# Table work in a Fourier transform's stage: scalings on ScalarE, the norm's variance product later, table pieces dealt out evenly

## The chip, the cores and the metric

The kernel runs on one core of one Trainium2 chip, in float32. The metric is the device time of one execution in microseconds, as the median of several runs. The trace is that of one execution, taken by the hardware profiler.

A core has five engines, each with its own in-order queue: TensorE (PE) multiplies matrices, VectorE (DVE) and ScalarE (ACT) work element by element, GpSimd (POOL) does the same more slowly and issues transfers, SyncE (SP) issues transfers. They wait for each other on semaphores.

## The reference, cut to what matters

The input `x` is [16, 16, 256, 256]: batch, channels, rows, columns. Two layers follow each other. The second, a convolution block, is not touched by the change. The first is a Laplace neural operator on a group-normalised `x`:

```python
alpha = jnp.fft.fft2(x, axes=(-2, -1))
A = 1.0 / (omega1[:, None, None, None] - weights_pole1[None])
Bm = 1.0 / (omega2[:, None, None, None] - weights_pole2[None])
S = jnp.einsum('ikpq,oikp,xikq->oxik', weights_residue, A, Bm)
output_residue1 = jnp.einsum('biox,oxik->bkox', alpha, S)
C = jnp.einsum('biox,oikp->bikpx', alpha, A)
D = jnp.einsum('bikpx,xikq->bikpq', C, Bm)
output_residue2 = jnp.einsum('bikpq,ikpq->bkpq', D, weights_residue)
x1 = jnp.fft.ifft2(output_residue1, s=(Ny, Nx), axes=(-2, -1)).real
E1 = jnp.exp(weights_pole1[..., None] * tyc)
E2 = jnp.exp(weights_pole2[..., None] * txc)
```

`x1` plus a product of `output_residue2` with `E1` and `E2` is added to `x`. What depends on the poles alone (`A`, `Bm`, `E1`, `E2` and products of them with the residues) does not depend on `x`: these are the tables. They are computed on the chip, in DRAM tensors `td` (residues times `Bm`), `avd` (`A`, in planes) and `ed` (the exponentials).

## The kernel before, in words

Four stages run one after the other: `layer0_forward`, `layer0_mix`, `layer0_back`, `layer1`. All that is changed lies in `layer0_forward` and in `tables`, which it calls. `layer0_mix` reads `td` and `avd`, `layer0_back` reads `ed`.

**Steps.** The forward transform has 64 steps, one for each of 16 batches times four groups of four channels. Step i does the following. `fetch` has loaded the four channels two steps before, and VectorE has taken their statistics (L174, L176). `halves` of the next step makes the group norm's numbers and `eo`, the sums and differences of the upper and the lower half of the rows: one on VectorE (L191), one on POOL (L194). `rows` runs twice, for two channels each; it multiplies `eo` with the Fourier matrix of the rows (`pu`, L207) and with the first poles' table (`pv`, L214). ScalarE copies one half of `pu` (`right`, L222), VectorE adds and subtracts it (`u`, L224), and ScalarE scales `pv` by the norm's factor `rs` (`v`, L231). `poles` multiplies `v` with the second poles' table (`pd`, L241); VectorE multiplies with the residues (L252), and POOL sums up. `columns` then transforms the columns of the batch before: products `px` (L313), evictions with a scale on ScalarE (`o`, L320), and stores issued by POOL (L329). Three groups of channels have two calls of `columns` with four evictions, the fourth has three calls with five. At a batch's end `finish` closes the residues' sums (L278, L286).

**The norm.** `group_norm_scalars` is a generator with two products on TensorE: the mean (L34), from which VectorE makes the negative mean and the squares `q` (L36 to L39), and, after a `yield`, the variance (L42), followed by an addition (L44), a square root on ScalarE (L46, which needs its own table set) and six small VectorE operations up to `rs` (L53). `halves` runs through it and yields at the same places; the main loop calls `next` before the first `rows`, between the two `rows`, and after the second.

**Tables.** `tables` is one generator. It makes first 16 residue pieces (one for each k: six VectorE operations of 256 columns, L415 to L420, eight small ones, L426, and then four products on TensorE, an eviction and a store), then 33 plane pieces in eleven triples (ten VectorE operations each, L466 to L490, and a store), then 16 exponential pieces (arguments L515, reduction L517 to L522, a sine on ScalarE L523 with its own table set, scaling L525, the exponential by a polynomial L769 to L783, and the rest to L534, with a store). From step 4 on, the loop asks for one piece at the end of each step, 43 in all; the last is asked for at step 46.

**What sets the order.** The block runs under `tc.manual_schedule` for TensorE alone: its instructions stand in the program's order. Those of VectorE, ScalarE, POOL and SP are put in order by a planner, which works with priorities and estimated durations and can run ahead of the program's order when an engine seems free. Semaphores come from data and buffer dependencies. Tables have one buffer for each tile name (`tp`, `bufs=1`); `pu`, `pv` and `px` have two PSUM buffers each; `z` three, `eo` two.

Of the kernel before, what the change touches and what calls it, by code (L numbers as in the profile page):

```python
# [18 lines left out]
C = 16  # L19
# [53 lines left out]
def layer0_forward(ctx, tc, d, al, bd, tabs):  # L73
# [105 lines left out]
    def halves(b, cg, z, mv):  # L179
# [5 lines left out]
        yield from group_norm_scalars(nc, sm, psn, ones, mv, 2, nm, rs)  # L185
# [9 lines left out]
        yield eo, rs  # L195

# [139 lines left out]
    with tc.manual_schedule(engines={mybir.EngineType.PE}):  # L336
# [3 lines left out]
        *_, ready = halves(*steps[0], *fetched.pop(0))  # L340
        pieces = tables(ctx, tc, d, psx, tabs)
        acc = rsc = None
        for i, (b, cg) in enumerate(steps):
            now, following = ready, iter(())
            if i + 1 < len(steps):
                following = halves(*steps[i + 1], *fetched.pop(0))
                next(following)
            v0 = rows(b, cg, 0, *now)
            next(following, None)
# [3 lines left out]
            ready = next(following, None)  # L353
# [5 lines left out]
            poles(cg, (v0, v1), acc)  # L359
            if b:  # L360
                for g0 in range(8 * cg, 8 * cg + 8 if cg < 3 else NF, 4):
                    columns(b - 1, g0, rsc)
            if i + 2 < len(steps):
                fetched.append(fetch(*steps[i + 2]))
            if i >= 4:
                next(pieces, None)
# [16 lines left out]
def tables(ctx, tc, d, psum, tabs):  # L383
# [5 lines left out]


    krow = load(nc, cp, d["krow_t"], [P, N], "krow_t")
    w = frequencies(nc, cp, d["tx"], krow, [P, N], "wt")
    sign = load(nc, cp, d["sign_t"], [P, 1], "sign_t")
    qr = cp.tile([P, C], F32, name="tqr")
    qi = cp.tile([P, C], F32, name="tqi")
    rr = cp.tile([P, C, M], F32, name="trr")
    ri = cp.tile([P, C, M], F32, name="tri")
    for t in range(2):
        ps = slice(64 * t, 64 * t + 64)
        nc.sync.dma_start(out=qr[ps], in_=d["p2r_iq"])  # L400
        nc.sync.dma_start(out=qi[ps], in_=d["p2i_iq"])
        nc.sync.dma_start(out=rr[ps], in_=d["rr_iq"])
        nc.sync.dma_start(out=ri[ps], in_=d["ri_iq"])
    nc.vector.tensor_scalar(qi, qi, sign, None, ALU.mult)
    nri = cp.tile([P, C, M], F32, name="tnri")
    nc.vector.tensor_scalar(nri, ri, sign, None, ALU.mult)
    nc.vector.tensor_scalar(ri, nri, -1.0, None, ALU.mult)
    q2 = cp.tile([P, C], F32, name="tq2")
    nc.vector.tensor_tensor(q2, qr, qr, ALU.mult)
    mt = load(nc, cp, d["mt"], [P, 2, 16], "mt")  # L410
    for k in range(C):
        e = tp.tile([P, N], F32, tag="te", name="te")
        r = tp.tile([P, N], F32, tag="trec", name="trec")
        br = tp.tile([P, N], F32, tag="tbr", name="tbr")
        nc.vector.tensor_scalar(e, w, qi[:, k : k + 1], None, ALU.add)  # L415
        nc.vector.tensor_tensor(r, e, e, ALU.mult)
        nc.vector.tensor_scalar(r, r, q2[:, k : k + 1], None, ALU.add)
        nc.vector.reciprocal(r, r)
        nc.vector.tensor_scalar(br, r, qr[:, k : k + 1], -1.0, ALU.mult, ALU.mult)
        nc.vector.scalar_tensor_tensor(e, e, -1.0, r, ALU.mult, ALU.mult)  # L420
        wts = []
        for h in range(2):
            wt = tp.tile([P, 2, 2, 16, M], F32, tag=f"wt{h}", name="wt")
            shape = [P, 16, M]
            for part, c, coef in ((0, 0, rr), (0, 1, ri), (1, 0, nri), (1, 1, rr)):
                nc.vector.tensor_tensor(  # L426
                    wt[:, part, c],
                    mt[:, h].unsqueeze(2).to_broadcast(shape),
                    coef[:, k].unsqueeze(1).to_broadcast(shape),
                    ALU.mult,  # L430
                )
            wts.append(wt)
        yield
        ps = psum.tile([P, 2, N], F32, tag="px", name="pt")
        for h, wt in enumerate(wts):
            for part, rhs in ((0, br), (1, e)):
                nc.tensor.matmul(
                    ps[:, h],
                    lhsT=wt[:, part].rearrange("p c i m -> p (c i m)"),
                    rhs=rhs,  # L440
                    start=part == 0,
                    stop=part == 1,
                )
        t = tp.tile([P, 2, N], F32, tag="tt", name="tt")
        nc.scalar.copy(t, ps)
        nc.sync.dma_start(out=td[:, :, k], in_=t)

    krow = load(nc, cp, d["krow_m"], [P, N], "krow_m")  # L450
    w = frequencies(nc, cp, d["ty"], krow, [P, N], "wm")
    sign = load(nc, cp, d["sign_m"], [P, 1], "sign_m")
    pr = cp.tile([P, 32], F32, name="tpr")
    pi = cp.tile([P, 32], F32, name="tpi")
    for q in range(4):
        nc.sync.dma_start(out=pr[32 * q : 32 * q + 32], in_=d["p1r_ip"])
        nc.sync.dma_start(out=pi[32 * q : 32 * q + 32], in_=d["p1i_ip"])
    nc.vector.tensor_scalar(pi, pi, sign, None, ALU.mult)
    pr2 = cp.tile([P, 32], F32, name="tpr2")
    nc.vector.tensor_tensor(pr2, pr, pr, ALU.mult)  # L460
    npr = cp.tile([P, 32], F32, name="tnpr")
    nc.vector.tensor_scalar(npr, pr, -1.0, None, ALU.mult)
    for g in range(NF):
        four = [P, 32, 4]
        e = tp.tile(four, F32, tag="ae", name="ae")
        nc.vector.tensor_tensor(  # L466
            e,
            w[:, 4 * g : 4 * g + 4].unsqueeze(1).to_broadcast(four),
            pi.unsqueeze(2).to_broadcast(four),
            ALU.add,  # L470
        )
        r = tp.tile(four, F32, tag="ar", name="ar")
        nc.vector.tensor_tensor(r, e, e, ALU.mult)
        nc.vector.tensor_tensor(r, r, pr2.unsqueeze(2).to_broadcast(four), ALU.add)
        nc.vector.reciprocal(r, r)
        av = tp.tile([P, 32, 4, 3], F32, tag="av", name="av")
        half = [64, 32, 4]
        nprb = npr.unsqueeze(2)
        nc.vector.tensor_tensor(av[:64, :, :, 1], r[:64], nprb[:64].to_broadcast(half), ALU.mult)
        nc.vector.tensor_tensor(av[64:, :, :, 1], r[64:], e[64:], ALU.mult)  # L480
        nc.vector.scalar_tensor_tensor(
            av[:64, :, :, 0].rearrange("p k f -> p (k f)"),
            e[:64].rearrange("p k f -> p (k f)"),
            -1.0,
            r[:64].rearrange("p k f -> p (k f)"),
            ALU.mult,
            ALU.mult,
        )
        nc.vector.tensor_tensor(av[64:, :, :, 0], r[64:], nprb[64:].to_broadcast(half), ALU.mult)
        nc.vector.tensor_scalar(av[:, :, :, 2], av[:, :, :, 0], -1.0, None, ALU.mult)  # L490
        nc.sync.dma_start(out=avd[g], in_=av.rearrange("p k f l -> p (k f l)"))
        if g % 3 == 2:
            yield


    phase = load(nc, cp, d["phase"], [P, 1], "phase")
    turn = cp.tile([P, 1], F32, name="turn")
# [4 lines left out]
    for i, axis in enumerate("12"):  # L502
# [7 lines left out]
        for k in range(0, C, 2):  # L510
# [16 lines left out]
            if axis == "2":  # L527
                nc.vector.tensor_scalar(n, n, last, None, ALU.mult)
# [971 lines left out]
```

## Time and profile before

| | |
|---|---|
| median of three runs | 7309.22 us (7302.86 to 7325.03) |
| profiled execution, its own time | 7312.28 us |
| its span | 7310.5 us |
| forward transform in it, up to the first matmul of the mix | 1384.24 us |
| PE / PEld / DVE / ACT / POOL busy | 6750.3 / 3787.1 / 4970.2 / 3811.4 / 3470.0 us |
| granted TensorE clock, mean over the span | 0.969 of full speed |

In the forward transform (the first 1376 us) the groups of instructions that the change touches are these. Times are busy times in us over the stage, and means in ns of one.

| line | engine, tile | count | busy | mean |
|---|---|---|---|---|
| L42 | PE, `gn_var` | 128 | 22.5 | 245 |
| L46 | ACT, `gnr` | 64 | 13.0 | 203 |
| L46, L523 | ACT, loads of a table set | 17, 16 | 21.8, 20.5 | 1283 |
| L415, L417, L419 | DVE, residue scalings of 256 columns | 16 each | 5.4, 7.6, 5.8 | 336, 475, 365 |
| L490 | DVE, third plane, 128 columns | 33 | 11.7 | 356 |
| L515, L525 | DVE, arguments' scalings of 256 columns | 32 each | 10.4, 10.1 | 341, 351 |
| L528 | DVE, last scaling of 512 columns | 8 | 3.8 | 479 |
| L437 | PE, `pt` | 128 | 39.7 | 405 and 379 |
| L207, L214 | PE, `pu` and `pv` | 2048 each | 426.8, 413.3 | 292, 285 |
| L222 | ACT, `right`, 256 columns | 256 | 95.0 | 372 |

Float32 products show as two matmul records for each instruction of the program. A page's row gives the busy time of a group and, beside it, how long the engine had been idle just before its members and what ended that. An engine that is busy nine tenths of a slice sets the pace there; one that has two or three tenths does not, unless others wait for it. In an answer on waits the columns are the engine and line that waited, what it waited for, us in total, times, and the longest.

### The profile page before, as it was taken

The numbers are of one execution on the slowest core, as the hardware profiler recorded it, in microseconds if no ns is written. First come the engines' busy times: TensorE is split into PE (matmuls) and PEld (weight loads), VectorE is DVE, ScalarE is ACT, GpSimd is POOL, SyncE is SP. The second block draws the span as 40 slices with busy tenths as digits, with TensorE's granted clock in tenths as the row PEclk, the third lists the DMA queues.
The fourth block names the chain that finished last, engine by engine and source line by source line (L and its number), as shares of the span: only waits on it lengthen the run. The fifth ranks groups of instructions, "written<-read, shape, count | busy, mean of one in ns | idle before, by whom it ended". The sixth has DMA issues, their size and how long they took to land.

```text
span 7310.5 us, 147410 instructions
## 1 busy us (share of the span) xinstructions
PE 6750.3 (92%) x57640; PEld 3787.1 (52%) x57640; DVE 4970.2 (68%) x9465; ACT 3811.4 (52%) x5915; POOL 3470.0 (47%) x4612
## 2 busy tenths in 40 slices
PE   7889999899999998999789999999999999999997
PEld 5777778666667776777433333333333333333332
DVE  8999975466666665888666666666666666666662
ACT  2223333466666665222366666666666666666662
POOL 2334445322222222666554666556665555655663
PEclk9889999999999999999899999999999999999998
DMA  3344444433333333999767888888888888888886
GB/s 100 112 115 125 119 125 125 124 100 97 96 94 98 99 99 107 321 327 326 227 195 218 249 256 257 249 259 248 267 260 243 253 248 268 253 247 254 252 267 219
DMA packets 716089, 1443.59 MB, mean 197 GB/s; under 512 B 98954, under 2 KB 525254, under 8 KB 673638
## 3 DMA queue, kind: packets, MB, share of 16 engines
q1 hardware_dynamic: 567206, 959.76, 43.8%
q0 software_dynamic: 148192, 474.40, 20.9%
q8 instruction: 460, 7.54, 0.4%
q14 instruction: 231, 1.89, 0.1%
HBM read 877.12 MB, written 556.47 MB: 196 GB/s over the span
## 4 chain that ended last, share of the span: by engine, by line
PE 71%; DVE 16%; DMA 4%; ACT 4%; issue 3%; POOL 1%; SPq 0%; DVEq 0%; ACTq 0%; POOLq 0%
PE c2ps L1173 18%; PE c L1029 12%; PE pd L1097 12%; PE ph L700 5%; PE ps L643 5%; PE pg L665 4%; PE px L313 3%; ACT wide L1077 3%; DVE alb L607 2%; PE pu L207 2%; PE pr L1056 2%; PE py L860 2%; PE pv L214 2%; PE py L861 2%; DVE u L224 2%
## 5 line engine op out<-in xcount | busy, mean ns | idle before, releaser
L1077 ACT ACTIVATE wide<-c,b 32x512 f32<-32x512 f32 x2176 | 1479.3, 680 | 354.2 <-PE c L1029 302.6
L1105 DVE TENSOR_TENSOR t<-pd,r 64x512 f32<-64x512 f32 x1088 | 744.3, 684 | 1287.8 <-PE pd L1097 1262.3
L1108 DVE TENSOR_TENSOR top<-pd,t 32x512 f32<-32x512 f32 x2176 | 1504.1, 691 | 53.7 <-DMA cf<-bot 1.2
L1173 PE MATMUL c2ps<-rows,c 128*32 128x512 f32 x12288 | 1391.9, 600 | 16.4 <-DMA rows<-cf 16.4
L1089 POOL COPY wide<-wide 32x1031 f32<-32x1031 f32 (+1 forms) x576 | 569.6, 989 | 1236.2 <-ACT wide L1077 1208.7
L1029 PE MATMUL c<-z,w 102*128 102x512 f32 x2048 | 1014.5, 628 | 139.2 <-ACT wide L1077 116.6
L1097 PE MATMUL pd<-wide,dw 128*128 128x512 f32 x2048 | 1013.1, 617 | 6.0 <-ACT r L1065 2.9
L1173 PEld LDWEIGHTS c2ps<-rows,c 128*32 128x32 f32 x12288 | 400.3, 109 | 972.0 <-issue 891.6
L720 POOL DMA_DIRECT2D hd<-h x512 | 324.3, 640 | 1198.7 <-DVE h L713 1174.1
L1029 PEld LDWEIGHTS c<-z,w 102*128 102x128 f32 x2048 | 401.5, 198 | 676.5 <-issue 486.9
L1097 PEld LDWEIGHTS pd<-wide,dw 128*128 128x128 f32 x2048 | 377.1, 194 | 613.6 <-issue 447.5
L1182 ACT ACTIVATE e<-c2ps,b 128x512 f32<-128x512 f32 x256 | 176.0, 687 | 831.1 <-PE c2ps L1173 828.4
L1090 POOL COPY wide<-wide 32x1031 f32<-32x1031 f32 (+1 forms) x576 | 573.0, 995 | 36.1
L700 PE MATMUL ph<-ix,yt 64*128 64x256 f32 x4128 | 502.3, 390 | 7.2 <-issue 6.6
L643 PE MATMUL ps<-tt,lt 128*64 128x256 f32 x4224 | 495.5, 384 | 12.6 <-DMA tt<-td 10.0
L313 PE MATMUL px<-wxn,u 128*64 128x256 f32 x4224 | 481.9, 379 | 8.0 <-ACT o L320 7.9
L207 PE MATMUL pu<-fy,eo 128*128 128x128 f32 x2048 | 426.8, 292 | 26.8 <-DVE u L224 21.8
L700 PEld LDWEIGHTS ph<-ix,yt 64*128 64x128 f32 x4128 | 393.1, 190 | 94.0 <-issue 46.8
L1048 ACT ACTIVATE bot<-c,b 128x512 f32<-128x512 f32 x544 | 344.3, 684 | 175.2 <-PE c L1029 167.9
L873 POOL TENSOR_TENSOR x<-x,o 128x512 f32<-128x512 f32 x256 | 324.4, 1267 | 216.6 <-DVE o L872 198.5
L607 DVE TENSOR_SCALAR alb<-alc,m 128x1024 f32<-128x1024 f32 x330 | 419.9, 1396 | 0.0
L214 PE MATMUL pv<-at,eo 128*128 128x128 f32 x2048 | 413.3, 285 | 0.0
(204 smaller groups left out, 10418.6 us busy)
## 6 DMA issues: line engine op xcount, KB each, us to landing
rows<-cf SPq DMA_DIRECT2D x128, 2176.0 KB
z<-zn SPq DMA_DIRECT2D x768, 257.8 KB
cf<-top POOLq DMA_DIRECT2D x512, 240.0 KB, 7.0
cf<-bot POOLq DMA_DIRECT2D x96, 840.0 KB, 11.6
alc<-al SPq DMA_DIRECT2D x264, 256.0 KB
zn<-zb SPq DMA_DIRECT2D x128, 516.0 KB
o<-zn SPq DMA_DIRECT2D x128, 516.0 KB
z<-in_x SPq DMA_DIRECT2D x64, 1024.0 KB
```

The costliest lines, as they stand in the source:

```text
L207: nc.tensor.matmul(pu[:, xh, e].rearrange("p v m -> p (v m)"), lhsT=lhs, rhs=fy[:, e], start=True, stop=True,)
L313: nc.tensor.matmul(ps[64 * k : 64 * k + 64, :, h], lhsT=u[:, h, part, g0 + j + k].rearrange("p f c -> p (f c)"), rhs=wxn[:, h, part], star ...
L643: nc.tensor.matmul(ps[64 * h : 64 * h + 64, v], lhsT=lt[:, h, k, 1 - v : 3 - v].rearrange("p l f c -> p (l f c)"), rhs=tt[:, h, k], start= ...
L700: nc.tensor.matmul(ph[q][:, e], lhsT=yt[lanes, i].rearrange("p t k -> p (t k)"), rhs=ix[lanes, i], start=n == 0, stop=n == 3,)
L1029: nc.tensor.matmul(ps[:, a], lhsT=w, rhs=z[:k, c : c + 2, 0:N], start=True, stop=True)
L1077: nc.scalar.activation(self.feat[64 - 32 * q : 96 - 32 * q, f, self.groups[g], :H], ps[q][32 * f : 32 * f + 32], AF.Mish, bias=b1[0][32 * ...
L1089: nc.gpsimd.tensor_copy(flat[0:32, f, 1:m], flat[64:96, f, 0 : m - 1])
L1090: nc.gpsimd.tensor_copy(flat[96:128, f, 0 : m - 1], flat[32:64, f, 1:m])
L1097: nc.tensor.matmul(ps, lhsT=dwt if self.tail else dw, rhs=self.feat[:, f, cs, :H], start=True, stop=True,)
L1105: nc.vector.tensor_tensor(t[64:128], ps[:64], self.r[:, cs], ALU.mult)
L1108: nc.vector.tensor_tensor(self.top[32 * f : 32 * f + 32, cs, q], ps[lanes], t[lanes], ALU.add)
L1173: nc.tensor.matmul(ps[32 * j : 32 * j + 32], lhsT=c2[:, blk, dx, :], rhs=t[:, 4 * j + blk : 4 * j + blk + 4, x : x + H], start=(blk, dx) = ...
```

## The change

Three things are changed, all in the forward transform.

1. **Variance product.** `halves` takes only the first part of `group_norm_scalars` before it makes `eo`, and goes through the rest after it has yielded `eo`. The loop takes the first yield before the first `rows` and the second after `poles`. So on TensorE the variance product stands behind the second poles' products of the step, in front of the columns, and not between the two halves of the rows.
2. **Scalings.** Seven of the VectorE operations of the tables become ScalarE activations: two additions of a per-partition number (`Identity` with a bias), and multiplications by a per-partition number or by -1 (`Copy` with a scale). One small VectorE operation is new (`nqr`, once).
3. **Pieces.** `tables` now has three generators, `residues`, `planes` and `exponentials`, whose pieces are merged by their place in their own list. There are 65 pieces, planes one by one. Steps 4 to 63 take one each, and steps 4, 16, 28, 40 and 52 two. The operations inside a piece are otherwise the same.

```diff
@@ halves
-        yield from group_norm_scalars(nc, sm, psn, ones, mv, 2, nm, rs)
+        scalars = group_norm_scalars(nc, sm, psn, ones, mv, 2, nm, rs)
+        next(scalars)
...
         yield eo, rs
+        yield from scalars
@@ layer0_forward, main loop
-        *_, ready = halves(*steps[0], *fetched.pop(0))
+        ready, _ = halves(*steps[0], *fetched.pop(0))
...
-                next(following)
+                ready = next(following)
             v0 = rows(b, cg, 0, *now)
-            next(following, None)
             if b and cg == 0:
                 rsc = finish(b - 1, acc)
             v1 = rows(b, cg, 1, *now)
-            ready = next(following, None)
...
             poles(cg, (v0, v1), acc)
+            next(following, None)
...
-            if i >= 4:
+            for _ in range(0 if i < 4 else 2 if i % 12 == 4 else 1):
                 next(pieces, None)
@@ tables: residues()
+        nqr = cp.tile([P, C], F32, name="tnqr")
+        nc.vector.tensor_scalar(nqr, qr, -1.0, None, ALU.mult)
...
-        nc.vector.tensor_scalar(e, w, qi[:, k : k + 1], None, ALU.add)
+            nc.scalar.activation(e, w, AF.Identity, bias=qi[:, k : k + 1])
...
-        nc.vector.tensor_scalar(r, r, q2[:, k : k + 1], None, ALU.add)
+            nc.scalar.activation(r, r, AF.Identity, bias=q2[:, k : k + 1])
...
-        nc.vector.tensor_scalar(br, r, qr[:, k : k + 1], -1.0, ALU.mult, ALU.mult)
+            nc.scalar.activation(br, r, AF.Copy, scale=nqr[:, k : k + 1])
@@ tables: planes()
-        nc.vector.tensor_scalar(av[:, :, :, 2], av[:, :, :, 0], -1.0, None, ALU.mult)
+            nc.scalar.activation(av[:, :, :, 2], av[:, :, :, 0], AF.Copy, scale=-1.0)
...
-        if g % 3 == 2:
-            yield
+            yield
@@ tables: exponentials()
-                nc.vector.tensor_scalar(arg[:, j], tr, pi[:, k + j : k + j + 1], None, ALU.mult)
+                    nc.scalar.activation(arg[:, j], tr, AF.Copy, scale=pi[:, k + j : k + j + 1])
...
-                nc.vector.tensor_scalar(arg[:, j], tr, pr[:, k + j : k + j + 1], None, ALU.mult)
+                    nc.scalar.activation(arg[:, j], tr, AF.Copy, scale=pr[:, k + j : k + j + 1])
...
-                nc.vector.tensor_scalar(n, n, last, None, ALU.mult)
+                    nc.scalar.activation(n, n, AF.Copy, scale=last)
@@ tables: end
+    parts = ((residues(), C), (planes(), NF), (exponentials(), C))
+    order = sorted(((i + 0.5) / n, p) for p, (_, n) in enumerate(parts) for i in range(n))
+    for _, p in order:
+        next(parts[p][0])
         yield
+    for part, _ in parts:
+        for _ in part:
+            pass
```

## The prediction

> **What bounds the kernel now.** I read the page's slices first, to see where in the span the changed code runs. All of it runs in the forward transform, the first seven and a half of the 40 slices (one slice is 7310.5 / 40 = 183 us).
>
> ```profile
> PE   7889999899999998999789999999999999999997
> DVE  8999975466666665888666666666666666666662
> ACT  2223333466666665222366666666666666666662
> PEclk9889999999999999999899999999999999999998
> ```
>
> VectorE (DVE) is at nine tenths in slices 1 to 4, then falls to 7, 5, 4. ScalarE (ACT) has two or three tenths throughout. The granted TensorE clock is lower in slices 1 and 2. So the stage begins bound by VectorE and ends bound by TensorE.
>
> The chain of waits repeats itself in time, so I took step boundaries from the first matmul of the second poles (`pd`, L241) in the timeline: step 5 begins at 163.9, step 36 at 851.3, step 62 ends at 1332.6. Busy times in those windows (columns: window, length, then busy us and count of PE, PEld, DVE, ACT, POOL, then clock, DMA share, GB/s):
>
> ```profile
> 1075.80:1283.10 207.30, 207.30 (x2031) 172.03 (x2030) 121.45 (x375) 68.25 (x136) 107.68 (x150) 1.00 0.45 121
> 163.90:851.30 687.40, 603.80 (x5375) 503.10 (x5374) 635.52 (x1774) 221.50 (x399) 284.22 (x389) 0.94 0.43 119
> 851.30:1332.60 481.30, 467.75 (x4545) 386.74 (x4544) 334.60 (x942) 168.37 (x318) 241.09 (x334) 1.00 0.43 116
> ```
>
> The first line is twelve steps with no table work left: PE is busy all the time, 207.3 / 12 = 17.28 us a step (three of 16.66, one of 19.09), and DVE needs 121.45 / 12 = 10.12. In steps 5 to 35 a step takes 687.4 / 31 = 22.2 us, 20.5 of it DVE; DVE is idle 51.9 us in all, 1.7 a step. Steps 36 to 62 are PE-bound except ten that still carry exponentials (481.3 against 27 bare steps at 464).
>
> Why does DVE idle where it bounds? The waits of 163.9 to 1040.1:
>
> ```profile
> PE gn_var L42 <- DVE gnq L39: 62.6, 21, 5.3
> PE pu L207 <- DVE u L224: 20.2, 20, 1.9
> PE px L313 <- ACT o L320: 7.2, 4, 1.9
> ...
> DVE u L224 <- ACT right L222: 25.8, 27, 1.5
> DVE arg L515 <- DMA ed<-arg: 17.0, 7, 3.6
> DVE arg L525 <- ACT n L523: 10.5, 12, 1.8
> ```
>
> PE's largest wait is the norm's variance product, which stands in the middle of a step's row products and needs a DVE result that is queued behind table work. While PE waits there, it makes no `pu`; afterwards DVE waits for the copy of the next `pu` (25.8 us). The timeline at such a place:
>
> ```profile
> 286.44 0.49 PE L42 MATMUL gn_var<-gnq,ones 128*128 128x2 f32 x2 [4.26 <-DVE gnq L39]
> 286.99 0.77 PE L207 MATMUL pu<-fy,eo 128*128 128x128 f32 x2
> ...
> 290.72 0.39 PE L207 MATMUL pu<-fy,eo 128*128 128x128 f32 x2
> ```
>
> After 4.26 us of waiting the pairs start 0.43 us apart and reach 0.22 only from 290 on.
>
> **What the Trainium skill says.** "TensorE: Matmul & The Clock Gate", section "HAM oscillation — how this bites in real kernels": gaps of more than about 3.4 us put the array back to half rate. The pairs above, 0.43 against 0.22 us, and the mean clock of 0.94 in steps 5 to 35 against 1.00 later agree. "SBUF — State Buffer", section "Who interferes with whom": VectorE operations with two SBUF inputs or in a two-port mode are shut out while GpSimd works; PE and ACT never are. The trace agrees: L52, 143 ns at best, takes up to 2341 ns, about one `eo` subtraction on POOL (L194, 2433 ns). So a scaling moved to ScalarE also escapes that lock.
>
> **The change part by part.**
>
> *Scalings.* DVE loses, by rows of the groups (us in total): L415 5.4, L417 7.6, L419 5.8, L490 11.7, L515 10.4, L525 10.1, L528 3.8, together 54.8 us of instruction time in 152 instructions net. Neighbours overlap, so it is less in busy time. Rows and medians of all table work in steps 5 to 35 give 349.6 us where the windows show 635.5 - 31 x 10.12 = 321.8: a factor 0.92, so about 50 us. ScalarE gains 112 ops of 256 columns (L222's copy of that size: 372 ns, 42 us), 33 of 128 columns and 8 of 512 (about 0.3 and 0.63 us: 15 us). It is busy 221.5 of 687.4 us there, so its 57 us lie in idle time; without that cover they would cost 0.9 us a step. No table-set load is added: the built program has 33 in this stage, as before, 1283 ns each.
>
> *Spreading.* The diff puts one piece a step, but only PE keeps program order; on DVE the planner decides. In the built program it still runs ahead: plane pieces are done by step 27, exponentials by step 35 (before: 19 and 45); only residue pieces, tied to their PE products, reach step 62. With the same medians, table work falls on DVE as follows: steps 0 to 4, 15.6 us (before 10.2); steps 5 to 35, 333.0 (349.6); steps 36 to 62, 32.6 (72.5). So the gain is no halving of a bound: a heavy block (steps 5 to 19, 231.7 to 179.5 us) is levelled into a lighter one.
>
> *The variance product.* It goes behind the sixteen `pd` products, with columns (6.9 us of `px` for four) before the next step's rows. PE stops waiting for `gnq` in the rows. Added is a new order on ScalarE: the square root (L46) now stands before the step's evictions of `px`. If DVE is late with `gnv`, four evictions queue behind it, and PE, having two `px` buffers, stops after 3.5 us of columns; the next `gn_mean`, and DVE's `gnq`, wait in turn. Likewise L422 (needs DVE's square) stands before `right`, and the arguments' scaling (L521) waits for the table's store (3.5 to 3.9 us on the chain) with `right` behind it; it used to be DVE that waited there (17.0 us).
>
> *Sums, against the profiled span.* Steps 5 to 35: DVE busy 31 x 10.12 + 0.92 x 333.0 = 620 us, 20.0 a step; PE needs 17.5. Idle is the unknown. Below, 0: 620 us. Above, with the present 1.7: 673. From the waits, DVE loses about 60 us in the 41 steps to 1040, 1.45 a step; without the 25.8 of the row stalls it is 0.85, and I add something for ScalarE's new round trips: 1.0 a step, 651 us, a gain of 36. Steps 36 to 62: PE bound, 464 + 7.5 residue pieces x 0.86 (eight products of 256 columns at 0.108, px's 6.91 us for 64) = 470.5, a gain of 11. Steps 0 to 4 are DVE-bound and get 5.4 us more table work: a loss of 5. Sum: 42 us faster.
>
> *Costed at nothing.* DMAs: as many stores as before (33 plane, 16 residue, 16 exponential) on SP's queue, but residue stores now stand before later input fetches. A fetch is two steps ahead of use, which hides it; if a store blocks the queue it costs up to the 5.8 us of one late `z`. The last residue product and its store come before nine columns (26 us of `px`), so the next stage's load, issued at 1375 and awaited 10.0 us, stays where it is. Instructions of later stages are unchanged in order.
>
> **The rivals.**
> 1. *The stall only moves.* ScalarE's in-order waits (L46 before evictions, L422 and L521 before `right`) give DVE back what the rows gave: idle 1.7 to 2.3 a step, 673 to 691 us. With +11 and -5 that is 2 to 20 us faster: no change to speak of. For it: 146 or so new crossings; 0.3 us each would be 44 us. Against: in the built order one to three other DVE instructions, 0.8 us or more, stand between most requests and their use.
> 2. *PE becomes the bound.* With the clock at 1.00, steps 5 to 35 near DVE's 620 us and port collisions fewer: 60 to 80 us faster, 7229 to 7249.
> 3. *Slower.* The same square root, but in a loop: DVE late with `gnv`, evictions late, columns stop, `gn_mean` late, DVE dry before `gnq`, gap over 3.4 us, half rate again. It loses 22 us once steps 5 to 35 take 687 + 22 + 11 - 5 = 715, i.e. idle of 95 / 31 = 3.1 us a step, twice today's. From two table loads behind `gnv` (2 x 1.28) and an eviction that would be reached: 7331 or more. Against: PE holds two column groups in hand, and DVE has four BN statistics of 0.67 us and table work to do meanwhile.
> 4. *The planner's front-loading eats it*: more late planes wait for their store (3.0 us on the chain) because one buffer holds `av`. This belongs to rival 1 in time.
>
> **How the numbers follow.** The profiled run took 7312.3 against a median of 7309.2, within their spread, so I subtract 42 from the median: 7267. A difference under 0.3% (22 us) can't be told from none. Forecast (idle 0.5 to 1.5, 7251 to 7282): 0.60. Rival 1 with 4: 0.22. Rival 2: 0.10. Rival 3: 0.08. Faster is forecast, rival 2 and a little of rival 1: 0.72; same: 0.19; slower: 0.09. The range leaves out rival 3 and the far end of rival 2: 7230 to 7305.
>
> **What would show it.** Right: `gn_var`'s wait for `gnq` near nothing; clock 0.98 or more in steps 5 to 35; DVE near 20 us of 21 a step there; PE full from step 36; exponentials ended by step 35. Wrong: waits of `px` on `o`, or of `o` on the square root, of tens of us; DVE waiting on `te`, `trec` or `arg` from ScalarE; `right` late behind L521; steps 5 to 35 over 673 us.

## The result, and the profile after

The changed kernel takes 7323.11 us (median of 12 runs, 7306.53 to 7338.07), the kernel before in the same comparison 7321.65 us (12 runs, 7302.86 to 7336.68): a ratio of 1.0005 with a 95% interval of 0.9994 to 1.0017. There is no difference. The forecast was 42 us less, and the time lies above the forecast's range.

The profiled execution of the changed kernel has a span of 7311.9 us. Its busy tenths in 40 slices:

```profile
PE   6888999899999998999789999999999999999997
DVE  8998755466666665888666666666666666666662
ACT  2444433466666665222366666666666666656662
PEclk9999999999999999999889999999999999999998
```

Slices 1 to 4 (the first is slice 0) show what was meant: ScalarE has four tenths where it had two or three, VectorE comes down a slice earlier, and the granted clock is nine tenths in slices 1 and 2. Yet the stage isn't shorter. Cut at the same places as in the prediction (first `pd` product of a step, now L243):

| boundary or window | before | after | forecast |
|---|---|---|---|
| step 5 begins | 163.9 | 172.6 | 5 later |
| steps 5 to 35 | 687.4 | 656.7 | 651 |
| steps 36 to 62 | 481.3 | 503.0 | 470.5 |
| first product of the mix | 1384.2 | 1385.0 | 42 earlier |

So 30.7 us were won in steps 5 to 35, and 8.7 lost ahead of them and 21.7 behind. The windows of the changed kernel (window, length, then busy us and count of PE, PEld, DVE, ACT, POOL, clock, DMA share, GB/s); the last is a step without table work:

```profile
172.60:829.30 656.70, 586.12 (x5309) 476.29 (x5308) 603.96 (x1660) 277.06 (x527) 284.58 (x389) 0.97 0.43 122
829.30:1332.30 503.00, 489.05 (x4604) 400.53 (x4602) 290.85 (x894) 167.52 (x332) 237.79 (x334) 0.99 0.41 112
1051.90:1068.80 16.90, 16.90 (x166) 13.96 (x164) 10.20 (x30) 5.58 (x12) 8.02 (x11) 1.00 0.42 111
```

VectorE works 603.96 us in steps 5 to 35, less than the forecast 620, but it idles 52.7 us, 1.7 a step, as before. In steps 36 to 62 PE alone is busy for 489.05 us, where 470.5 were to be the whole length, and a bare step takes 16.90 us instead of 16.66.

The waits of steps 5 to 35 of the changed kernel (us in total, times, longest):

```profile
PE pu L209 <- DVE u L226: 51.6, 24, 4.6
...
DVE u L226 <- ACT right L224: 17.8, 22, 1.8
PE px L315 <- ACT o L322: 16.1, 19, 1.7
```

The wait of `gn_var` for `gnq` (62.6 us in the prediction's list) is gone. In its place PE waits for `u`, that is for a free `pu` buffer, 51.6 us, where that wait came to 20.2 us over a longer window before. No other wait of PE or VectorE is of that size in this window.

Step 46 of the changed kernel, one of the seven of steps 36 to 62 that carry a residue piece, in the timeline (start, us, engine and line):

```profile
1020.99 0.70 PE L442 MATMUL pt<-tbr,wt 128*128 128x256 f32 x2
...
1021.52 0.59 PE L442 MATMUL pt<-te,wt 128*128 128x256 f32 x2
...
1022.16 0.23 DVE L431 TENSOR_TENSOR wt<-mt,trr 128x64 f32<-128x64 f32 x1 [3.86 <-PE pt L442]
...
1022.82 0.28 PE L34 MATMUL gn_mean<-mv,ones 128*128 128x2 f32 x2
...
1025.05 1.75 DVE L423 RECIPROCAL trec<-trec 128x256 f32<-128x256 f32 x1
...
1027.62 1.89 DVE L226 TENSOR_TENSOR u<-pu,right 128x256 f32<-128x256 f32 x4
...
1028.78 0.46 PE L209 MATMUL pu<-fy,eo 128*128 128x128 f32 x2 [2.01 <-DVE u L226]
```

The four `pt` products take from 1020.99 to 1022.82, 1.83 us. VectorE, after 3.86 us without work, begins its next eight `wt` at 1022.16, when `pt` has released their first buffer, and does the rest of the piece (reciprocal included) ahead of its first `u` at 1027.62, while PE fills both `pu` buffers and stops for 2.01 us. Such a step takes 20.9 us against 16.9: a residue piece costs 4.0 us here. The seven steps with a piece take 3.2 to 5.6 us more than bare ones, 30.5 together. The two dearest are steps 50 and 61, with 22.5 us each: their mean granted clock is 0.92, where the other five have 1.00.

And the variance product's new place, in a bare step of the changed kernel, then the same place of the kernel before:

```profile
1051.96 2.04 PE L243 MATMUL pd<-bt,v 128*64 128x128 f32 x32
1053.93 0.38 PE L42 MATMUL gn_var<-gnq,ones 128*128 128x2 f32 x2
1054.24 7.13 PE L315 MATMUL px<-wxn,u 128*64 128x256 f32 x64
```

```profile
1075.82 2.04 PE L241 MATMUL pd<-bt,v 128*64 128x128 f32 x32
1077.68 7.08 PE L313 MATMUL px<-wxn,u 128*64 128x256 f32 x64
```

From `pd` to `px` it is 2.28 us instead of 1.86. Before, the product stood among the row products, and the two starts around it lay 0.37 us apart where 0.22 is usual:

```profile
1088.36 0.39 PE L214 MATMUL pv<-at,eo 128*128 128x128 f32 x2
1088.59 0.28 PE L42 MATMUL gn_var<-gnq,ones 128*128 128x2 f32 x2
1088.73 0.47 PE L207 MATMUL pu<-fy,eo 128*128 128x128 f32 x2
```

In the waits between 103 and 172 us of the changed kernel stands what step 5's late start begins with. The four waits lie in steps 0 to 3, where no batch is complete and there are no columns to transform:

```profile
PE gn_mean L34 <- DVE gnv L44: 6.9, 4, 2.5
```

The second of them, in the timeline:

```profile
118.20 0.38 PE L34 MATMUL gn_mean<-mv,ones 128*128 128x2 f32 x2 [2.55 <-DVE gnv L44]
...
120.28 0.64 PE L216 MATMUL pv<-at,eo 128*128 128x128 f32 x2
120.71 0.63 PE L209 MATMUL pu<-fy,eo 128*128 128x128 f32 x2
```

Soon after this wait of 2.55 us, and after one of 2.01 us at 143.88, the row products start 0.43 us apart instead of 0.22, for 3 to 4 us each time. From 102.6 to 153.8 the mean clock is 0.93; in the same steps of the kernel before it was 1.00. So of the 8.7 us only 4.7 are more idle time of PE; the other 4.0 are more busy time for about as many products.

### The profile page after: what moved, and what is told of

The parts are those of the page before. It is cut to its first block, busy times and chain, and to the rows that moved or that the text cites. A ratio compares the mean times of both kernels' runs of the same rounds, so it can differ in the third digit from the quotient of the medians.

```text
span 7311.9 us, 147432 instructions
## 1 busy us (share of the span) xinstructions
PE 6761.3 (92%) x57640; PEld 3780.1 (52%) x57640; DVE 4894.8 (67%) x9313; ACT 3868.0 (53%) x6068; POOL 3461.9 (47%) x4612
## 3 DMA queue, kind: packets, MB, share of 16 engines
q0 software_dynamic: 148192, 474.40, 20.9%
## 4 chain that ended last, share of the span: by engine, by line
PE 74%; DVE 14%; ACT 4%; issue 3%; DMA 3%; SPq 0%; POOL 0%; DVEq 0%; ACTq 0%; POOLq 0%
PE c2ps L1188 18%; PE c L1044 13%; PE pd L1112 13%; PE ph L715 5%; PE ps L658 5%; PE px L315 4%; PE pg L680 4%; ACT wide L1092 3%; DVE alb L622 2%; PE pu L209 2%; PE pr L1071 2%; PE pv L216 2%; PE py L875 2%; PE py L876 2%; PE pt L696 1%
## 5 line engine op out<-in xcount | busy, mean ns | idle before, releaser
L1188 PE MATMUL c2ps<-rows,c 128*32 128x512 f32 x12288 | 1392.4, 600 | 11.8 <-DMA rows<-cf 11.8
L315 PE MATMUL px<-wxn,u 128*64 128x256 f32 x4224 | 488.0, 381 | 16.6 <-ACT o L322 16.6
L331 POOL DMA_DIRECT2D al<-o x544 | 323.2, 606 | 207.4 <-ACT o L322 188.6
```

The lines of the kernel that those rows point to most:

```text
L315: nc.tensor.matmul(ps[64 * k : 64 * k + 64, :, h], lhsT=u[:, h, part, g0 + j + k].rearrange("p f c -> p (f c)"), rhs=wxn[:, h, part], star ...
L1188: nc.tensor.matmul(ps[32 * j : 32 * j + 32], lhsT=c2[:, blk, dx, :], rhs=t[:, 4 * j + blk : 4 * j + blk + 4, x : x + H], start=(blk, dx) = ...
```

## The experiments

From these readings came the theory: the work was taken away, but what counts is where in a step the rest of it stands. A step has a rows phase (first `pu` to first `pd`), in which VectorE must make the norm's numbers, half of `eo` and eight `u` in time for two `pu` buffers, and a columns phase, in which PE works without VectorE. Summed over steps 5 to 35, the rows phase went from 356.1 to 309.6 us and the columns phase from 331.3 to 347.1. The rivals: the planner's front-loading ate the gain; waits for single buffers; stores in the wrong queue; chance of one profile. Times are given as step 5's start, steps 5 to 35, steps 36 to 62, first product of the mix, in us of one profile; the changed kernel has 172.6, 656.7, 503.0, 1385.0. "Table work" is all that `tables` issues.

### The variance product's place

The changed kernel with part 1 undone:

```diff
             v0 = rows(b, cg, 0, *now)
+            next(following, None)
...
             poles(cg, (v0, v1), acc)
-            next(following, None)
...  halves, and the call behind the second rows, as in the kernel before
```

> The changed kernel with the variance product back between the two halves of the rows; scalings on ScalarE and even pieces stay. Windows by the first second-pole product: changed kernel, steps 5 to 35 took 656.7 us and steps 36 to 62 took 503.0. My theory: the product's old place costs TensorE less in a bare step (16.66 and 19.09 us, not 16.90 and 19.44), so steps 36 to 62 drop by 27 x 0.27 = 7 us to 496; in steps 5 to 35 TensorE waits for the squares again, tens of us, and they take 675 to 700. Rival: that wait was never worth anything because VectorE bounds those steps; then they stay within 5 us of 657 and the whole is 7 us faster than the changed kernel.

Measured: ratio to before 0.9988 [0.9978, 0.9998]; 164.7, 669.6, 489.2, 1374.1. Its steps 36 to 62:

```profile
834.40:1323.60 489.20, 479.12 (x4603) 398.06 (x4602) 300.22 (x906) 170.60 (x337) 238.16 (x334) 1.00 0.43 115
```

The early steps get their 8 us back, steps 36 to 62 another 13.8, about half of it in bare steps (16.66 and 19.09 us again) and the rest in steps with a piece (mostly 19.8, that is 3.1 for a piece), and steps 5 to 35 lose 12.9, less than if the wait for `gnq` had been worth its 62.6 us: that wait returns with 9.1 us only. Net, part 1 makes the stage 11 us slower here, in one profile of each.

Part 1 alone, on the kernel before:

> The kernel before with the variance product behind the second poles and nothing else. The prediction's step: waits of the product for the squares (62.6 us) vanish, VectorE's idle time in steps 5 to 19 falls from 2.1 to about 1 us a step, 15 us. Against it bare steps now cost 0.27 us more, 64 x 0.27 = 17 us. So the forward transform stays within 8 us of 1384. Rival, that the wait held TensorE up for its full 62.6 us: 1340 or less.

Measured: 1.0006 [0.9999, 1.0014]; 177.6, 678.5, 483.4, 1389.1. The same picture: 9 us won in steps 5 to 35, 14 lost ahead of them, 2 behind (bare steps take 16.90 and 19.44 here too).

The changed kernel with the product ahead of the poles' products instead of behind them:

```diff
+            next(following, None)
             poles(cg, (v0, v1), acc)
-            next(following, None)
```

> The changed kernel with the variance product in front of the second poles' products, right after the rows, and not behind them. My theory: 0.24 us a bare step is what a product with 128 columns of weights costs between products with 64 columns; beside the rows' products of 128 columns it costs less, so bare steps fall from 16.90 to 16.66 to 16.75 and steps 36 to 62 to about 497 us; steps 5 to 35 stay within 6 us of 657. Rival: the product costs the same at any place that is not between pv and pu; bare steps stay at 16.90.

Measured: 1.0020 [1.0013, 1.0027]; 166.8, 681.3, 494.0, 1394.3. Bare steps take 16.5 and 19.0, so the price of the place between `pd` and `px` is confirmed, and the early wait is gone. But steps 5 to 35 lose 24.6 us, all in the rows phase (357.8), and the wait for `u` rises to 80.9 us. PE is busy for 586.9 us there, as in the changed kernel, so that the loss is idle time. The planner has put VectorE's work in another order; that this is the cause, and which instruction does the harm, was not settled.

### The scalings

Part 2 undone in the changed kernel (the seven activations are VectorE operations again):

> The changed kernel with the seven scalings back on VectorE; the variance product behind the second poles and even pieces stay. My theory: VectorE gets 50 us of busy time back, nearly all in steps 5 to 35, which take 685 to 700 us, and steps 36 to 62 get 1.2 us more work before the first u of each step with a residue piece, 510 us. Rival: ScalarE's round trips cost what they save; then steps 5 to 35 stay within 8 us of 657 and steps with a residue piece get shorter than 20.9.

Measured: 0.9999 [0.9991, 1.0008]; 175.1, 648.6, 502.6, 1379.4.

```profile
175.10:823.70 648.60, 586.90 (x5309) 479.74 (x5308) 618.67 (x1765) 227.15 (x401) 285.61 (x389) 0.97 0.45 123
```

VectorE works 14.7 us more than in the changed kernel, and the window is 8.1 us shorter. Here the scalings on ScalarE bought nothing: what they save VectorE was lost again elsewhere. The hand-overs between the two engines are the likely place (VectorE's wait for `arg` from ScalarE, 10.5 us in the changed kernel, is gone), but this was not shown one by one.

Part 2 alone, on the kernel before:

> The kernel before with the seven scalings on ScalarE and nothing else. The prediction's step (50 us of VectorE's busy time saved where VectorE bounds): steps 5 to 35 take 650 to 660 us (687.4 before) and the forward transform ends at 1345 to 1360 (1384.2). Rival, that the scalings save nothing because VectorE waits for ScalarE's answers: 1376 or more.

Measured: 0.9987 [0.9979, 0.9995]; 163.8, 684.8, 477.2, 1375.0.

```profile
163.80:848.60 684.80, 603.46 (x5374) 501.08 (x5373) 618.31 (x1679) 275.46 (x537) 283.49 (x389) 0.95 0.43 119
848.60:1325.80 477.20, 466.20 (x4545) 385.65 (x4544) 308.16 (x888) 168.43 (x327) 238.30 (x334) 1.00 0.44 117
```

The busy time saved is the forecast's: 635.5 - 618.3 and 334.6 - 308.2, together 43 us in the two windows, against 50. The stage gets 9 us shorter. The rest becomes idle time of VectorE, part of it in front of results that now come from ScalarE (its wait for `arg` is 20.6 us over the stage, 3.4 the longest).

### The spreading

Part 3 alone, on the kernel before:

> The kernel before with the pieces merged and dealt out and nothing else (scalings on VectorE, variance product between the rows). If levelling VectorE's load is what gains: steps 5 to 35 take 665 to 680 us, steps 36 to 62 some 490 (bare steps at 16.66, with a residue piece at 20 to 21), the forward transform 1370 to 1380. Rival, that it only moves the residues' products from steps where TensorE has time to steps where it has none: 1385 or more.

Measured: 1.0001 [0.9992, 1.0009]; 166.1, 672.5, 493.8, 1383.3. It wins 14.9 in steps 5 to 35 and gives back 12.5 in steps 36 to 62, to which it moves residue pieces.

The changed kernel with every piece held until its own step. A piece's first operation gets a zero made of that step's norm, so that the planner can't run ahead:

```diff
+    def gate(src, shape, name):
+        zero = tp.tile([P, 1], F32, tag=f"{name}z", name=f"{name}z")
+        nc.vector.tensor_scalar(zero, step["now"][:, 0:1], 0.0, None, ALU.mult)
+        t = tp.tile(shape, F32, tag=name, name=name)
+        nc.vector.tensor_scalar(t, src, zero, None, ALU.add)
+        return t
...
-            nc.scalar.activation(e, w, AF.Identity, bias=qi[:, k : k + 1])
+            qk = gate(qi[:, k : k + 1], [P, 1], "rgate")
+            nc.scalar.activation(e, w, AF.Identity, bias=qk)
...  planes and exponentials likewise
```

> The changed kernel with every table piece tied to its step: two tiny VectorE operations a piece add zero times the step's norm to one of its inputs, so the planner can't start it before that step (in the built program plane pieces then end at step 62 and not 27, exponentials at 62 and not 35). Theory A, front-loading: the gain was lost because the planner did not spread; with 16.4 us of VectorE and 18.0 of TensorE in each step, steps 5 to 62 take some 1100 us (1159.7 now), the forward transform to the first product of the mix 1325 to 1340 (1385.0 now). Theory B, the pieces' crossings and bursts cost the same wherever they stand: steps 5 to 62 stay over 1140 us.

Measured: 1.0053 [1.0036, 1.0071]; 169.1, 641.9, 549.9, 1414.3.

```profile
169.10:810.90 641.80, 580.85 (x5309) 470.41 (x5308) 513.09 (x1451) 234.07 (x455) 286.80 (x389) 0.98 0.42 117
810.90:1360.90 550.00, 498.37 (x4606) 403.69 (x4604) 439.76 (x1243) 210.46 (x408) 246.37 (x334) 0.99 0.41 111
```

This is the even load that the change's words promise: VectorE 16.6 and 16.3 us a step, PE 18.7 and 18.5, and neither is full in either window. Yet the stage is 29 us slower. So sums of a step don't decide it, and that front-loading ate the gain is not borne out. The gates are not free, though: VectorE works 58 us more in the two windows than in the changed kernel, in 140 more instructions, and at most 7 us of that had stood in steps 0 to 4. A gate also puts a piece right behind the norm. How much of the 29 us is due to the gates was not measured.

The changed kernel with residue pieces dealt out twice as fast, so that two instead of seven fall into steps 36 to 62:

```diff
-    order = sorted(((i + 0.5) / n, p) for p, ...
+    order = sorted(((i + 0.5) / n / (1 if p else 2), p) for p, ...
```

> The changed kernel with the residue pieces merged at half their places, so that in the built program the last one's VectorE work stands in step 41 and not 62. My theory: a residue piece costs 4.0 us in a TensorE-bound step (1.8 of products, 2.0 of late u), and 4 to 5 pieces fewer stand there, so steps 36 to 62 fall from 503 to 482 to 488; in steps 5 to 35 they cost VectorE 3.9 us each, so these rise by 12 to 20 us from 656.7, and the first product of the mix stays within 10 us of 1385. Rival, that the loss after step 36 comes from the variance product's place alone: steps 36 to 62 stay over 497.

Measured in one execution: 7322.48 us; 175.2, 675.1, 483.9, 1387.3.

```profile
175.20:850.30 675.10, 600.92 (x5351) 490.01 (x5350) 618.23 (x1715) 286.19 (x547) 285.64 (x389) 0.96 0.43 120
850.30:1334.20 483.90, 478.24 (x4565) 390.89 (x4564) 275.43 (x839) 158.40 (x312) 237.75 (x334) 1.00 0.42 113
```

Five pieces fewer make the late window 19.1 us shorter (3.8 a piece) and the early one 18.4 longer (3.7 a piece). A residue piece costs about 3.8 us in either window of the changed kernel. At that price, as an estimate, the eight pieces that the change took out of steps 5 to 35 (16 before, 8 after) come to some 30 us, as much as was won there in all; in exchange the exponentials of the late steps moved in.

### Buffers, and the phase of the work

The changed kernel with two buffers for the residue pieces' tiles:

```diff
-            e = tp.tile([P, N], F32, tag="te", name="te")
+            e = tp.tile([P, N], F32, tag="te", name="te", bufs=2)
...  tbr, wt0 and wt1 likewise
```

> The changed kernel with two buffers each for a residue piece's te, tbr and two wt tiles. My theory: a residue piece in the TensorE-bound steps costs 4 us because VectorE stands idle until the piece before has been multiplied (wt waits for pt, 32.8 us in steps 36 to 62) and then has 5 us of work before the first u; with two buffers that wait falls under 5 us, the step with a piece falls from 20.9 to about 18.7 us (only the products' 1.8 us left), and steps 36 to 62 take about 489 us. Rival: the cost is the products and the queue on ScalarE, not the buffer; then they stay at 500 or more.

Measured: 0.9969 [0.9959, 0.9979]; 174.5, 632.1, 497.9, 1354.9.

```profile
174.50:806.60 632.10, 579.34 (x5309) 468.60 (x5308) 589.13 (x1648) 272.39 (x522) 285.34 (x389) 0.98 0.45 126
```

The stage is 30 us shorter, but not where it was expected. In steps 36 to 62 only 5.1 come back: five of the seven steps with a piece still take 20.2 to 20.3 us, and VectorE's wait for `pt` is still 26.2 us (32.8 with one buffer). Why two buffers leave most of that wait was not found. The gain is 24.6 us in steps 5 to 35. There the rows phase falls from 309.6 to 291.1, PE's wait for `u` from 51.6 to 32.7, and the table work that VectorE does between a step's norm (L36) and its last `u`, summed over steps 5 to 35 of the traces, from 163 to 140 us.

Next, table work held until the columns phase: two buffers as above, the gate on the step's products with the residues (ready when the columns begin) instead of the norm, and the exponential cut in three, 97 pieces in all.

```diff
-            poles(cg, (v0, v1), acc)
+            step["now"] = poles(cg, (v0, v1), acc)
...
-    parts = ((residues(), C), (planes(), NF), (exponentials(), C))
+    parts = ((residues(), C), (planes(), NF), (exponentials(), 3 * C))
```

> The changed kernel with two buffers for te, tbr and wt, every table piece tied to the residues' products of its step (so that it becomes ready when the columns begin and not when the rows begin), and an exponential piece cut in three: 97 pieces over 60 steps. In the built program 24 us of the table's VectorE time then stand between a step's norm and its last u, against 148 in the changed kernel. Theory C, the rows: a step loses time only through table work that VectorE does between the norm and the last u, because TensorE has but two pu buffers; the columns, 9.6 us with 4.2 of VectorE's own work, hide it. Then steps 5 to 62 take 1080 to 1110 us (1159.7 now, 1168.7 before), the first product of the mix comes at 1310 to 1335 (1385.0), and the median is some 60 us under before. Theory B, waits for ScalarE and in-order bursts cost the same wherever they stand: steps 5 to 62 stay over 1140.

Measured: 1.0003 [0.9993, 1.0012]; 173.3, 617.9, 543.6, 1386.1. The forecast for steps 5 to 62, 1080 to 1110 us, failed: they take 1161.5, as before this edit (1159.7). Steps 5 to 35 are 38.8 us shorter than in the changed kernel (rows phase 284.5, columns 333.4, table work between norm and last `u` 17 us), but steps 36 to 62, where there is more table work now, are 40.6 longer. New waits stand in the list: VectorE for `z`, 79.5 us over steps 5 to 62 against 33.2, and for `right`, 132.7 against 79.1.

The same with the variance product between the rows:

> As x_columns, with the variance product back between the two halves of the rows. If the rows carry no table work, VectorE has the squares ready there, and the product costs less: bare steps at 16.66 and 19.09 us, not 16.90 and 19.44. Theory C: 58 x 0.27 = 15 us faster than x_columns. Rival, that the wait for the squares returns: slower than x_columns by 10 us or more.

Measured: 0.9957 [0.9942, 0.9972]; 165.6, 611.9, 523.5, 1352.0, with a stage 34 us shorter than with the product behind the poles. One wait of it over steps 5 to 62:

```profile
DVE st L174 <- DMA z<-in_x: 67.7, 42, 3.9
```

And `x_columns` with the exponentials left whole, 65 pieces:

> As x_columns, with exponential pieces whole and 65 pieces. In the built program 110 us of table work stand in the rows again. Theory C: every microsecond of it beyond about 1 a step is lost there, so steps 5 to 62 take 40 to 60 us more than in x_columns. Theory B: the same as x_columns within 15 us.

Measured in one execution: 7344.28 us; 174.5, 629.5, 545.0, 1402.7. Against `x_columns` it is 13 us longer in steps 5 to 62, where the theory of the rows wanted 40 to 60. In steps 5 to 35 there are 57 us more of table work between norm and last `u` (74 against 17), and the rows phase is only 11.8 us longer (296.3). So cutting the long pieces is worth little, and a microsecond of table work in the rows costs far less than one.

### The stores' queue

To see whether the wait for `z` is the tables' stores in front of the fetches on SP's queue, the changed kernel with `td` and `avd` stored by ScalarE's queue and `ed` by POOL's:

```diff
-            nc.sync.dma_start(out=td[:, :, k], in_=t)
+            nc.scalar.dma_start(out=td[:, :, k], in_=t)
...  avd likewise; ed on nc.gpsimd
```

> The changed kernel with the stores of the tables off SP's queue: planes and residues issued by ScalarE, which makes them, exponentials by POOL. If input fetches late behind stores cost time, VectorE's wait of the statistics for z (32.7 us in steps 5 to 60) falls under 10 us and the first product of the mix comes 10 to 25 us earlier than 1385. If that wait is time in which VectorE would have waited for TensorE anyway, 1380 to 1390.

Measured: 1.0023 [1.0014, 1.0033]; 174.6, 652.4, 503.3, 1386.9. The wait for `z` is 32.6 us, as without it. The stage is the same, and the stores were not what held the fetches up. The median is 17 us over the kernel before all the same. In the profile the time behind the first product of the mix is 5944.3 us against 5926.9, but without this edit, too, it lies anywhere from 5926.3 to 5941.7; what is lost there, and why, stays open. The same edit on `x_columns_var_back`:

> x_columns_var_back (two buffers, pieces tied to the columns and cut, variance product between the rows) with the stores off SP's queue as in x_stores. There VectorE waits 65.8 us for z in steps 5 to 60. If that wait is on the path: under 15 us of it left, steps 5 to 62 at 1095 to 1110 us (1135 in x_columns_var_back), first product of the mix at 1315 to 1330, median some 55 us under before. If not: within 8 us of x_columns_var_back's 1352.

Measured: 0.9987 [0.9979, 0.9995]; 165.2, 626.3, 530.3, 1376.6; the wait for `z` grows to 84.3 us, and the stage is 24.6 us longer than without the edit. The stores are not its cause. In the program the fetch of a `z` also waits until its buffer's last reader, `eo`, is done; that this is the cause was not shown.

### The same kernel once more, and a faster one

The changed kernel again, for what a profile varies by:

> The changed kernel once more, to see how far the stage times of one kernel agree from one profiled execution to the next: steps 5 to 35 within 5 us of 656.7, steps 36 to 62 within 3 us of 503.0, the first product of the mix within 6 us of 1385.0.

Measured in one execution: 7324.71 us; 174.0, 658.2, 505.3, 1389.9. Windows repeat within 2.3 us, the stage's end within 5, so the losses of 8.7 and 21.7 are not chance, and single differences of 3 us or less in a window, or of 5 in the stage's end, mean nothing. Only this kernel was profiled twice.

The changed kernel with two buffers and the variance product between the rows, that is with parts 2 and 3 only:

> The changed kernel with two buffers for te, tbr and wt, and the variance product back between the rows. If the two are separate causes, their gains add (30 and 11 us of the time to the first product of the mix): 1340 to 1347, a median 40 us under before. If both only reshuffle VectorE's order, 1355 to 1375.

Measured: 0.9949 [0.9929, 0.9969], 7280.93 us against 7319.84; 164.2, 642.7, 490.8, 1351.3. This is half a per cent faster than the kernel before, and the changed kernel was no faster than that one. The two edits alone moved the mix's start by 10.9 and 30.1 us, together by 33.7; they don't add up fully: with the product back, two buffers gain nothing in steps 36 to 62 (490.8 against 489.2 with one).

## Why the prediction was wrong

In the profiles the forecast is off by 43 us: 42 were to be won and 0.8 were lost. By its own sums (what is left, 1.1, lies between step 62 and the mix):

- **"Steps 36 to 62: PE bound, 464 + 7.5 residue pieces x 0.86": 32.5 us of the error; this is the step that failed.** PE bounds there, as said. Two terms of the sum were too small. *The piece*: 0.86 came from `px`'s rate, 0.108 us for a record of 256 columns. But `px` multiplies with 64 columns of weights, two such products for the two halves of the output's partitions, and `pt` with 128. A `pt` record takes 0.22 (the products, of two records each, start 0.53, then 0.43 us apart), so that a piece's four products, eight records, take 1.83 us. To that come 2.0 us in which PE waits for `u`: VectorE's residue work (some 3.8 us in the timeline, start to start: `wt` 1.4, square 0.3, reciprocal 1.7, `te` 0.3) falls ahead of the first `u`. With the rest of the step a piece costs 4.0, measured as 3.8 by moving five pieces away: 7 x (4.0 - 0.86) = 22 us. *The variance product*: costed at nothing in a bare step. It stands now between two groups of 64-column products and takes 0.24 (step of four evictions) to 0.35 us more than among 128-column ones: 27 x 0.27 = 7.3 us. The Trainium skill, "TensorEngine Tiling (Array Packing)", section "Key Properties", says that tiles work in parallel and that a change of the tiling mode drains the array. The rates 0.110 and 0.22 agree with the first; the 0.42 us from `pd` to `px` agree with the second, and putting the product back restored 16.66. *The clock*, which had no term here: the lower clock of steps 50 and 61 makes each 1.6 us longer than step 46, 3.3 us, about what remains.
- **"Steps 0 to 4 ... a loss of 5": 3.7 us of the error, and for another reason.** The 8.7 us are 4.7 of idle time and 4.0 of busy time, where the clock is lower. PE's waits of `gn_mean` for `gnv` come to 6.9 us. The norm's products share one PSUM buffer; behind the poles the variance has only the columns to hide in, and these steps have none. The prediction named the columns as cover and did not ask where they are missing. With the product between the rows again, or ahead of the poles, these waits are gone, and the clock is 1.00 in these steps.
- **"Steps 5 to 35 ... 1.0 a step, 651 us": 5.7 us off, from two errors that nearly cancel.** DVE's busy time was forecast at 620 and came to 604; idle time was to fall to 1.0 a step and stayed at 1.7. That the window came out near the forecast is luck. Why VectorE worked 16 us less was not found. Rival 1, "the stall only moves", was right in kind: the largest stall of PE moved from `gn_var` to `pu`. ScalarE's hand-overs, which that rival blamed, may have a part in it, since without them the window is 8.1 us shorter; PE's wait for `u` stays without them (54.3 us).
- **The scalings, "about 50 us"**: right as busy time, 43 in the two windows, with their cover on ScalarE as described. Wrong was to turn busy time into time one for one. Alone they bought 9 us, and taking them out of the changed kernel lost nothing. (One store of `ed` on the chain before took 4.22 us, more than the 3.5 to 3.9 that the prediction reads there; nothing hung on it.)
- **The spreading**: that the planner runs ahead was right, and so were "the exponentials ended by step 35". That this was the limit of the gain wasn't: the fully even version is slower.
- **What would show it**: the wait of `gn_var` near nothing was right; the clock 0.97 instead of 0.98; DVE 19.5 us of 21.2 a step, nearly as said; PE full from step 36, 489 of 503, but at a higher cost. The named danger, evictions behind the square root (16.1 us of `px` waiting for `o`), was small, and in steps 5 to 35 rival 3's half rate did not come: the clock rose from 0.94 to 0.97. It did come in steps 0 to 3 and in steps 50 and 61, after waits of 2.0 to 2.6 us, shorter than the 3.4 us that the prediction took from the Trainium skill ("TensorE: Matmul & The Clock Gate", section "HAM oscillation — how this bites in real kernels"); here the measurement decides. The length of the wait alone does not: steps 42, 46, 53 and 57 have the same 2.0 us and keep a clock of 1.00, and in the repeated profile it is steps 42, 50 and 61 that take 22.5 us.

Beyond the failed step, a reading that the runs support only in part: a step was summed up engine by engine, while a step has two phases, and only two `pu` buffers stand between them. That table work in the rows makes them longer is supported by the kernels with the product behind the poles (309.6, 291.1, 296.3 and 284.5 us of rows phase with 163, 140, 74 and 17 us of it in the changed kernel, `x_two_buffers`, `x_columns_whole` and `x_columns`), but not in proportion or even in order; and it is not the only cause, for the kernel before has 74 us of it there and 356.1 us of rows, in which `gn_var` waits. Open stay `x_var_ahead`'s order, the wait for `pt` that two buffers leave, the cause of the waits for `z`, and the later part of `x_stores`.

## What to carry to other kernels

Before turning saved busy time into saved time, look for the phase of a step in which others wait for that engine: here 43 us less work of VectorE shortened the stage by 9 us, and the version with an even load, gates included, was slower than the uneven one. Price a TensorE product by its own width of weights and by what stands on both sides of it, and before moving one for the sake of a wait, check in which steps the work that is to cover it doesn't exist. When work is moved from one stretch to another, count its price where it arrives as well as where it leaves: five residue pieces cost 3.8 us each in the steps that PE bounds, and 3.7 in the earlier ones.

## What was not expected of the hardware

- Float32 products with 128 columns of weights took 0.22 us for a record of 256 columns, pairs with 64 columns 0.110 a record (`pt` and `px`, both at a clock of 0.99 to 1.00).
- A product of two columns cost 0.42 us between `pd` and `px` and about 0.15 among the row products.
- Waits of PE of 2.0 to 2.6 us were in some cases followed by half rate (pairs 0.43 us apart instead of 0.22), for 3 to 4 us, and in others not.
- A version that leaves both engines unfilled (PE 580.85 and 498.37, VectorE 513.09 and 439.76 us of 641.8 and 550.0) was the slowest of those timed in several runs.
